# Four edits to an attention and expert kernel: an earlier Wo product, whole-tile key transposes, a head summed by parts, and weight loads queued behind gathered rows

## The chip, the cores and the metric

The kernel runs on one core of one Trainium2 chip. The metric is the device time of one execution in microseconds (us); for several runs it is their median. A core has five engines that work side by side and wait for one another by semaphores: PE (TensorE, the matrix products), DVE (VectorE), ACT (ScalarE), POOL (GpSimd) and SP (SyncE, which here only issues transfers). Transfers are issued on the queues of SP, ACT and POOL and are carried out by 16 DMA engines that all queues share.

## The reference

One layer: a linear-attention block with a data-dependent decay, then a mixture of twelve experts with two chosen per token, each with a residual and a layer norm. There are 2048 tokens of width 512, all in float32. Cut to what is computed:

```python
def attention(x):                       # heads of size 64, 8 of them
    xn = layernorm(x, gamma, beta)
    w = sigmoid(xn @ Wx @ Ww + bw)      # decay
    k, v, r = xn @ Wk, xn @ Wv, sigmoid(xn @ Wr)
    # per head, token after token:
    #   state = (1 - w_t)[:, None] * state + k_t[:, None] * v_t[None, :]
    #   y_t   = r_t @ state
    return y @ Wo

x = layernorm(x + attention(x))

def experts(x):
    probs = softmax(x @ gate_w.T)
    top_w, top_i = top_k(probs, 2); top_w /= top_w.sum()
    # out += (silu(x @ w1[e].T) * (x @ w3[e].T)) @ w2[e].T * weight of e for the token
    return out

x = layernorm(x + experts(x))
```

## The kernel before, in words

**Layout.** The tokens are taken in eight blocks of 256 (`TB`), each of two tiles of 128 rows; x stays in SBUF as `xs`. A tile has two chunks of 64 tokens (`L`), and inside a chunk the recurrence is unrolled into "levels" of block sizes 1, 2, ... 32: products of scaled queries and scaled keys, picked together by a mask. From chunk to chunk a state is carried.

**Head (lines 573 to 605).** Wx and Ww are multiplied into one matrix Wa, so that the decay needs one projection. SP first loads the first two tiles of x (line 71), then the four quarters of `ww` (line 579) in turn with `wxT` on ACT's queue (line 578), then Wk and the rest of x; Wr, Wv and Wo come on ACT's queue. PE then computes Wa by row tiles i: for each i, four quarters k, two passes each (float32 products show as two matrix instructions), into one PSUM tile that ACT copies out (line 597). So the first i already needs the last quarter. Ahead of i=2 the first block's normed rows are transposed (line 175), and after the loop a small product, `psl` (line 604), gives `lesser`, which the gate uses later.

**A block b (the loop at line 622).** PE's order is the program's order (a manual schedule for PE only); the orders on DVE, ACT, POOL and SP come from the framework's scheduler. PE does in turn: `mixed(1)` of the block before (`yp`, lines 353 and 354; ACT copies `yp` to `yT`, line 356), `levels(0)`, `residual` of the block before's second tile (`psp<-Wo,yT`, line 362; DVE adds it to `xs`, line 363, and takes statistics, lines 109 and 110), the three projections of the next block (line 197), the transposes of finished rows for the gate (`known.transpose`, line 395), `mixed(0)`, the gate's scores (`lg`, line 408), `levels(1)`, the small products of `known.place` (`pr`, line 455), `residual` of this block's first tile, the values (line 242), and the transposes of the block after next (line 175). `known.choose` is a chain of small DVE operations; `known.place` ends in indirect DMAs on POOL.

**levels (lines 288 to 343).** First the keys k64 are brought from (feature, token) to (token, feature): for each chunk c, pair of heads p and head h, a 64x64 product with the identity, into `kp` (line 296), which ACT copies to `kS` (line 300). Then 56 products per chunk give `pa` (line 316), which DVE turns into `A` (lines 318 and 321). Then `sp`, kS times the values (line 333), and two DVE operations per chunk form the new state (lines 340 and 341). `kp`, `sp` and one half of the transposes share one PSUM buffer; the projections, values, scores, `pr` and `residual` share two, in turn.

**scaled (line 255)** makes the scaled queries on DVE and ACT and the scaled keys on POOL, with two buffers per level.

**Experts (lines 801 to 958).** Experts 0 and 1 are fixed; the other ten are sorted by load and processed in that order as groups 3 to 12. Group 0 works on rows gathered during attention (`soon`), group 1 and 2 on the further rows of experts 1 and 0. Group g's body: gather the rows of group g+1 (`xg`, line 816, indirect DMAs on POOL), the hidden products (`psg`, line 845), the transposes of the gathered rows (`psx`, line 828), the output products of the group before (`pso`, line 874), each added into DRAM by an indirect DMA (line 879). The weights of one expert are a row of 2 MB; `ewp` holds three. The first two sorted experts' loads (line 929) are issued in the bodies of groups 0 and 1, later ones from group 3 on. `entries` (line 727) computes on DVE the row lists `come` of the sorted groups. At the end the sum is read back, normed and stored (lines 984 to 1000).

Of the kernel before, what the change touches and what calls it, by code (L numbers as in the profile page):

```python
# [16 lines left out]
P = 128  # L17
C = 512
# [34 lines left out]
def tile_kernel(ctx: ExitStack, tc: tile.TileContext, x, WxT, Ww, bw, Wk, Wv, Wr, Wo, gamma, beta, gate_wT, wall, same, masks, rev, cst, empty, ids, out):  # L53
# [13 lines left out]

    def load_x(i0, n):
        nc.sync.dma_start(xs[:, i0 : i0 + n, :], x[i0 * P : (i0 + n) * P, :].rearrange("(n p) d -> p n d", p=P))

    load_x(0, NTB)

    ident = const.tile([P, P], FP, tag="ident", name="ident")
    make_identity(nc, ident)
# [61 lines left out]
    with ExitStack() as att:  # L136
# [151 lines left out]
        def levels(n, S, qs, ks, vS, W):  # L288


            kp = ps_s.tile([P, 2, KT, HS], FP, tag="kp", name="kp")
            for c in range(2):
                for p in range(KT):
                    for h in range(2):
                        hp = slice(h * HS, (h + 1) * HS)
                        nc.tensor.matmul(  # L296
                            kp[hp, c, p, :], ks[L][hp, p, c * L : (c + 1) * L], ident[hp, hp], start=True, stop=True
                        )
            kS = lvl.tile([P, 2, KT, HS], FP, tag="kS", name="kS")
            nc.scalar.copy(kS, kp)  # L300

            A = []
            for c in range(2):
                cs = slice(c * L, (c + 1) * L)
                pa = ps_a.tile([P, KT, PAIRS], FP, tag="pa", name="pa")
                for p in range(KT):
                    for l in range(NL):
                        B = BLOCKS[l - 1] if l else 0
                        for h in range(2):
                            hp = slice(h * HS, (h + 1) * HS)  # L310
                            if l:
                                q = blocks(qs[B][hp, :, cs], B)[:, p, :, 1, :]
                                to = pa[hp, p, L + (l - 1) * L // 2 : L + l * L // 2].rearrange("p (i b) -> p i b", b=B)
                            else:
                                q, to = qs[0][hp, p, cs], pa[hp, p, 0:L]
                            nc.tensor.matmul(to, ks[B][hp, p, cs], q, start=True, stop=True)  # L316
                a = lvl.tile([P, KT, L], FP, tag="A", name="A", bufs=4)
                nc.vector.tensor_mul(a, pa[:, :, 0:L], eye.unsqueeze(1).to_broadcast([P, KT, L]))
                for l, B in enumerate(BLOCKS):
                    n_i = L // (2 * B)  # L320
                    nc.vector.copy_predicated(  # L321
                        blocks(a, B)[:, :, :, 1, :],
                        msk[:, l, :].rearrange("p (i b) -> p i b", b=B).unsqueeze(1).to_broadcast([P, KT, n_i, B]),
                        pa[:, :, L + l * L // 2 : L + (l + 1) * L // 2].rearrange("p q (i b) -> p q i b", b=B),
                    )
                A.append(a)

            sp = ps_s.tile([P, 2, KT, HS], FP, tag="kp", name="sp")
            for c in range(2):
                for p in range(KT):  # L330
                    for h in range(2):
                        hp = slice(h * HS, (h + 1) * HS)
                        nc.tensor.matmul(  # L333
                            sp[hp, c, p, :], kS[hp, c, p, :], vS[hp, 2 * n + c, p, :], start=True, stop=True
                        )
            states = [S]
            for c in range(2):
                new = p2.tile([P, KT, HS], FP, tag="state", name="state", bufs=6)
                whole = W[L].rearrange("p (q n) -> p q n", q=KT)[:, :, 2 * n + c : 2 * n + c + 1]
                nc.vector.tensor_mul(new, states[c], whole.to_broadcast([P, KT, HS]))  # L340
                nc.vector.tensor_add(new, new, sp[:, c, :, :])
                states.append(new)
            return A, states
# [229 lines left out]
        with ExitStack() as once:  # L573
            two = once.enter_context(tc.tile_pool(name="two", bufs=1))
            wxT = two.tile([P, KT, C], FP, tag="wxT", name="wxT")
            ww = two.tile([P, KT, C], FP, tag="ww", name="ww")
            for k in range(KT):
                nc.scalar.dma_start(wxT[:, k, :], WxT[k * P : (k + 1) * P, :])
                nc.sync.dma_start(ww[:, k, :], Ww[k * P : (k + 1) * P, :])
            load_w(nc.scalar, wsb["Wr"], Wr)  # L580
            load_w(nc.sync, wsb["Wk"], Wk)
            load_w(nc.scalar, wsb["Wv"], Wv)
            for i0 in range(NTB, NT, NTB):
                load_x(i0, NTB)
                if i0 == NTB:
                    load_w(nc.scalar, wsb["Wo"], Wo)
            xn = norm(0)
            with tc.manual_schedule(engines={PE}):
                for i in range(KT):
                    if i == 2:  # L590
                        xnT = transposed(xn)
                    ps = ps_p.tile([P, C], FP, tag="psp", name="psp")
                    for k in range(KT):
                        nc.tensor.matmul(
                            ps, wxT[:, k, i * P : (i + 1) * P], ww[:, k, :], start=(k == 0), stop=(k == KT - 1)
                        )
                    nc.scalar.copy(wsb["Wa"][:, i, :], ps)

                whole = const.tile([P, NE + NS], I32, tag="whole", name="whole")
                key, whole = whole[:, NE:].bitcast(FP), whole[:, 0:NE]  # L600
                lesser = const.tile([P, NE], FP, tag="lesser", name="lesser")
                ps = ps_p.tile([P, NE], FP, tag="psp", name="psl")
                for k in range(KT):
                    nc.tensor.matmul(ps, cc["ones"], gwT[:, k, :], start=(k == 0), stop=(k == KT - 1))
                nc.vector.tensor_scalar_mul(lesser, ps, -1.0)  # L605

        lvl = att.enter_context(tc.tile_pool(name="lvl", bufs=2))
        rt = att.enter_context(tc.tile_pool(name="rt", bufs=2))
# [4 lines left out]
        with tc.manual_schedule(engines={PE}):  # L613
# [8 lines left out]
            for b in range(NB):  # L622
                cur = kT, rT, aT, W
                tile0 = nxt
                if todo is not None:
                    yT = mixed(1, *todo)
                A0, states0 = levels(0, state, *tile0, vS, W)
                if b:
                    tile1 = scaled(1, *cur)
                else:  # L630
                    with tc.issue_after(ends[0]), tc.issue_after(ends[1]):
                        tile1 = scaled(1, *cur)
                if todo is not None:
                    residual(b * NTB - 1, yT)
                    known = Sorted((b - 1) * NTB, NTB)
                if b + 2 < NB:
                    with tc.issue_after(taken[-1]):
                        xn = norm(b + 2)
                if b + 1 < NB:
                    kT, rT, aT, W = decays_and_keys(xnT)  # L640
                    nxt = scaled(0, kT, rT, aT, W)
                ahead = b + 1 < NB
                if todo is not None and ahead:
                    known.transpose()
                yT = mixed(0, A0, states0, tile0[0][L], vS)
                if todo is not None and ahead:
                    known.score()
                    known.choose()
                A1, states1 = levels(1, states0[2], *tile1, vS, cur[3])
                state = states1[2]  # L650
                todo = A1, states1, tile1[0][L], vS
                if ahead:
                    if b:
                        known.place()
                    residual(b * NTB, yT)
                    vS = values(xnT)
                if b + 2 < NB:
                    xnT = transposed(xn)
                if b + 2 == NB:
                    proj.close()  # L660
                    soon = Soon(b * NTB)
# [139 lines left out]
    with ExitStack() as moe:  # L801
# [118 lines left out]
        groups += [Group(blocks(n), nth=r) for r, n in enumerate(SORTED)]  # L920
        weights = {(0, None): soon.w, (1, None): load_expert(1)}

        def load_sorted(r):
            if r < NS:
                weights[None, r] = w = ewp.tile([P, WROW], FP, tag="w", name="w")
                row = nc.values_load(
                    wix[0:1, r : r + 1], engines=(mybir.EngineType.SP,), min_val=0, max_val=(NE - 1) * P
                )
                nc.sync.dma_start(w, wall[bass.ds(row, P), :])

        xgT = gathered(soon.xg, groups[0].sizes)

# [3 lines left out]
        for g, group in enumerate(groups):  # L936
            ahead = groups[g + 1] if g + 1 < len(groups) else None
            if ahead:
                nxt = gather(ahead.source)
            if g < 2:  # L940
                with tc.issue_after(loaded.ins):
                    load_sorted(g)
            w = weights[group.expert, group.nth]
            h = hidden(w, xgT, group.N)
            if g == 0:
# [132 lines left out]
```

## Time and profile before

| what | us |
|---|---|
| median of 3 runs | 854.67 |
| lowest, highest | 853.89, 862.46 |
| the profiled execution, its own time | 855.35 |
| its span, first to last instruction | 853.6 |
| PE busy (share of the span) | 793.8 (93%) |
| head: first projection with Wa starts at | 26.36 |
| attention: blocks 0 to 7 up to about | 514 |
| experts: first hidden product of group 0 at | 533.31 |

How to read it: the profile is that of one execution. Its first part gives the busy time of each engine; the second cuts the span into 40 equal slices, with the share of each engine in tenths and the clock that PE was granted; the chain of waits goes back from the last instruction to what released each step, so its shares tell what set the end. Timelines list merged instructions by start, duration, engine, line, and "output<-inputs"; in square brackets stands how long the engine was idle before, and what it waited for. PE's durations of single products overlap (a product is 218 ns or more from its start to its end, while the next starts much earlier), so the pieces of the chain, not the sums of durations, are the cost of a stretch. PEld is the weight load that precedes each product.

### The profile page before, as it was taken

The numbers are of one execution on the slowest core, as the hardware profiler recorded it, in microseconds if no ns is written. First come the engines' busy times: TensorE is split into PE (matmuls) and PEld (weight loads), VectorE is DVE, ScalarE is ACT, GpSimd is POOL, SyncE is SP. The second block draws the span as 40 slices with busy tenths as digits, with TensorE's granted clock in tenths as the row PEclk, the third lists the DMA queues.
The fourth block names the chain that finished last, engine by engine and source line by source line (L and its number), as shares of the span: only waits on it lengthen the run. The fifth ranks groups of instructions, "written<-read, shape, count | busy, mean of one in ns | idle before, by whom it ended". The sixth has DMA issues, their size and how long they took to land.

```text
span 853.6 us, 18701 instructions
## 1 busy us (share of the span) xinstructions
PE 793.8 (93%) x7932; PEld 563.2 (66%) x7932; DVE 376.5 (44%) x1264; ACT 189.3 (22%) x400; POOL 247.2 (29%) x316
## 2 busy tenths in 40 slices
PE   6999999999999999999999999699999999999910
PEld 2778789789789788787886876474544544555500
DVE  2481763763665647547527456226212111111133
ACT  1231313212213213223132112011122211111104
POOL 3062302502504314224025004243243332212210
PEclk9999999999999999999999899799999999999965
DMA  9500000010010010010011224744265554645366
GB/s 331 188 2 1 3 21 32 3 51 2 3 50 2 3 50 3 3 50 3 2 51 26 102 100 141 252 104 155 56 177 135 136 130 145 162 130 137 45 198 225
DMA packets 25941, 72.78 MB, mean 85 GB/s; under 512 B 4033, under 2 KB 4193, under 8 KB 24305
## 3 DMA queue, kind: packets, MB, share of 16 engines
q1 hardware_dynamic: 14384, 48.44, 15.0%
q0 software_dynamic: 9312, 18.95, 12.0%
q10 hardware_dynamic: 2160, 4.19, 1.4%
q8 instruction: 62, 1.02, 0.5%
q14 instruction: 23, 0.18, 0.1%
HBM read 49.78 MB, written 21.99 MB: 84 GB/s over the span
## 4 chain that ended last, share of the span: by engine, by line
PE 89%; DMA 5%; DVE 2%; ACT 1%; issue 1%; ACTq 0%; POOL 0%; SPq 0%; POOLq 0%
PE psp L197 19%; PE psg L845 16%; PE pa L316 12%; PE pso L874 12%; PE psp L362 7%; PE psp L242 6%; PE psx L828 2%; PE yp L353 2%; PE sp L333 2%; PE kp L296 2%; PE yp L354 2%; PE lg L408 2%; DMA xg<-xd,src 2%; DMA xs<-in_x 2%; DVE st L109 1%; DMA acc<-y,to 1%
## 5 line engine op out<-in xcount | busy, mean ns | idle before, releaser
L845 PE MATMUL psg<-xgT,w 128*128 128x384 f32 (+4 forms) x480 | 141.0, 454 | 0.0
L845 PEld LDWEIGHTS psg<-xgT,w 128*128 128x128 f32 x480 | 91.5, 194 | 51.2 <-issue 13.9
L276 POOL TENSOR_TENSOR k<-kT,aT 128x256 f32<-128x256 f32 x16 | 16.4, 1026 | 307.0 <-ACT kT L226 228.6
L874 PE MATMUL pso<-w,h 128*128 128x512 f32 (+3 forms) x204 | 103.6, 627 | 0.0
L316 PE MATMUL pa<-q,k 64*64 64x32 f32 x2560 | 101.9, 221 | 1.3 <-issue 1.3
L316 PEld LDWEIGHTS pa<-q,k 64*64 64x64 f32 x2560 | 92.0, 137 | 1.4 <-issue 1.4
L859 DVE TENSOR_TENSOR sg<-sg,psg 128x384 f32<-128x384 f32 (+9 forms) x39 | 19.1, 490 | 157.1 <-ACT sg L857 157.1
L874 PEld LDWEIGHTS pso<-w,h 128*128 128x128 f32 (+3 forms) x204 | 31.1, 181 | 54.8 <-issue 54.0
L321 DVE COPY_PREDICATED A<-msk,pa 128x128 f32<-128x128 int32 x192 | 65.5, 341 | 3.7
L816 POOL DMA_INDIRECT xg<-xd,come x30 | 29.5, 984 | 125.6 <-PE psx L828 102.8
L879 POOL DMA_INDIRECT acc<-y,to x30 | 46.8, 1560 | 63.5 <-ACT y L878 57.5
L277 ACT COPY q<-q 128x256 f32<-128x256 f32 x96 | 40.0, 416 | 89.1 <-DVE q L275 41.2
L362 PE MATMUL psp<-Wo,yT 128*128 128x512 f32 x128 | 59.4, 607 | 0.0
L197 PE MATMUL psp<-xnT,Wa 128*128 128x256 f32 x256 | 56.8, 380 | 0.4 <-DVE lesser L605 0.4
L197 PE MATMUL psp<-xnT,Wr 128*128 128x256 f32 x256 | 56.6, 379 | 0.0
L197 PE MATMUL psp<-xnT,Wk 128*128 128x256 f32 x256 | 56.6, 379 | 0.0
L276 POOL TENSOR_TENSOR k<-k,W 128x256 f32<-128x256 f32 x80 | 54.5, 681 | 6.4
L242 PE MATMUL psp<-Wv,xnT 128*128 128x512 f32 x128 | 56.2, 592 | 0.0
L197 PEld LDWEIGHTS psp<-xnT,Wa 128*128 128x128 f32 x256 | 48.5, 190 | 9.6 <-issue 2.9
L197 PEld LDWEIGHTS psp<-xnT,Wk 128*128 128x128 f32 x256 | 48.6, 190 | 6.6
L197 PEld LDWEIGHTS psp<-xnT,Wr 128*128 128x128 f32 x256 | 48.6, 190 | 6.6
L269 DVE TENSOR_TENSOR q<-rT,aT 128x512 f32<-128x512 f32 x16 | 11.4, 711 | 79.9 <-ACT rT L232 77.7
(200 smaller groups left out, 1172.3 us busy)
## 6 DMA issues: line engine op xcount, KB each, us to landing
w<-in_wall SPq DMA_DIRECT2D x11, 2048.0 KB, 9.7
xs<-in_x SPq DMA_DIRECT2D x8, 512.0 KB, 12.3
xd<-xs SPq DMA_DIRECT2D x16, 256.0 KB, 2.5
acc<-xs SPq DMA_DIRECT2D x16, 256.0 KB, 2.6
xs<-acc SPq DMA_DIRECT2D x8, 512.0 KB, 6.4
out<-xs SPq DMA_DIRECT2D x8, 512.0 KB, 3.4
soon_w<-in_wall SPq DMA_DIRECT2D x1, 2048.0 KB
wxT<-in_WxT ACTq DMA_DIRECT2D x4, 256.0 KB, 5.4
```

Source lines behind the costliest of these rows:

```text
L197: nc.tensor.matmul(ps[:, j, :], wsb[w][:, k, m * P : (m + 1) * P], rhs[:, k, :], start=(k == 0), stop=(k == KT - 1),)
L242: nc.tensor.matmul(ps.rearrange("p q h j -> p (q h j)"), xnT[:, k, n * P : (n + 1) * P], wsb["Wv"][:, k, :], start=(k == 0), stop=(k == KT ...
L276: nc.gpsimd.tensor_mul(k_to[:, :, :, 0, :], k_from[:, :, :, 0, :], decay(B, 1))
L277: nc.scalar.copy(q_to[:, :, :, 0, :], q_from[:, :, :, 0, :])
L316: nc.tensor.matmul(to, ks[B][hp, p, cs], q, start=True, stop=True)
L321: nc.vector.copy_predicated(blocks(a, B)[:, :, :, 1, :], msk[:, l, :].rearrange("p (i b) -> p i b", b=B).unsqueeze(1).to_broadcast([P, KT, ...
L362: nc.tensor.matmul(ps, yT[:, k, :], wsb["Wo"][:, k, :], start=(k == 0), stop=(k == KT - 1))
L816: ins = nc.gpsimd.indirect_dma_start(xg[:n, j, :], None, xd[:, :], bass.IndirectOffsetOnAxis(ap=col[:n], axis=0))
L845: nc.tensor.matmul(ps[:, 0:N], w13[:, k, c0 : c0 + P], xgT[:, k, 0:N], start=(k == 0), stop=(k == KT - 1))
L859: nc.vector.tensor_mul(sg[:n, 0:N], sg[:n, 0:N], g)
L874: nc.tensor.matmul(ps[:m], h[:n, f, j * P : j * P + m], w2[:n, f, :], start=(f == 0), stop=(f == 2))
L879: add = nc.gpsimd.indirect_dma_start(acc[:, :], bass.IndirectOffsetOnAxis(ap=to[:m], axis=0), y[:m], None, compute_op=ALU.add).ins
```

## The change

1. **Head by parts.** The load of x's first rows is issued on SP behind the first quarter of `ww`. The products for Wa run with the quarters k outside and the row tiles i inside, into four accumulators at once (the two `pa` buffers, free at that time). The product for `lesser` follows quarter 1, the transposes of the first rows follow quarter 2, and the four copies to Wa follow all products.
2. **Keys by whole tiles.** `kp` is made by four 128x128 transposes, one for each pair of heads, instead of 64x64 products. Its layout is now (token of the tile, pair, head, feature), so four copies, two on DVE and two on ACT, bring the parts to `kS`, with the same layout as before.
3. **Wo product earlier.** `residual(b * NTB, yT)` of blocks 0 to 6 stands ahead of `levels(1)`, not behind it and `known.place`.
4. **First weights behind rows.** The loads of the first two sorted experts are both issued in the body of group 1, and each waits for the last gather issued till then (`queue`), that of group 2's rows.

```diff
-    load_x(0, NTB)
...
-            kp = ps_s.tile([P, 2, KT, HS], FP, tag="kp", name="kp")
+            kp = ps_s.tile([P, KT, 2, HS], FP, tag="kp", name="kp")
+            for p in range(KT):
+                nc.tensor.transpose(kp[:, p, :, :].rearrange("p h j -> p (h j)"), ks[L][:, p, :], ident)
+            kS = lvl.tile([P, 2, KT, HS], FP, tag="kS", name="kS")
             for c in range(2):
-                for p in range(KT):
-                    for h in range(2):
-                        hp = slice(h * HS, (h + 1) * HS)
-                        nc.tensor.matmul(
-                            kp[hp, c, p, :], ks[L][hp, p, c * L : (c + 1) * L], ident[hp, hp], start=True, stop=True
-                        )
-            kS = lvl.tile([P, 2, KT, HS], FP, tag="kS", name="kS")
-            nc.scalar.copy(kS, kp)
+                for h in range(2):
+                    copy = nc.scalar.copy if h else nc.vector.tensor_copy
+                    copy(kS[h * HS : (h + 1) * HS, c, :, :], kp[c * L : (c + 1) * L, :, h, :])
...
                 nc.sync.dma_start(ww[:, k, :], Ww[k * P : (k + 1) * P, :])
+                if k == 0:
+                    load_x(0, NTB)
...
+                ps = [ps_a.tile([P, 2, C], FP, tag="pa", name="psm") for _ in range(KT // 2)]
+                ps = [ps[i // 2][:, i % 2, :] for i in range(KT)]
+                for k in range(KT):
+                    for i in range(KT):
+                        nc.tensor.matmul(
+                            ps[i], wxT[:, k, i * P : (i + 1) * P], ww[:, k, :], start=(k == 0), stop=(k == KT - 1)
+                        )
+                    if k == 1:
...
+                        for n in range(KT):
+                            nc.tensor.matmul(psl, cc["ones"], gwT[:, n, :], start=(n == 0), stop=(n == KT - 1))
+                        nc.vector.tensor_scalar_mul(lesser, psl, -1.0)
+                    if k == 2:
+                        xnT = transposed(xn)
                 for i in range(KT):
-                    if i == 2:
-                        xnT = transposed(xn)
-                    ps = ps_p.tile([P, C], FP, tag="psp", name="psp")
-                    for k in range(KT):
-                        nc.tensor.matmul(
-                            ps, wxT[:, k, i * P : (i + 1) * P], ww[:, k, :], start=(k == 0), stop=(k == KT - 1)
-                        )
-                    nc.scalar.copy(wsb["Wa"][:, i, :], ps)
...
+                    nc.scalar.copy(wsb["Wa"][:, i, :], ps[i])
...
+                if ahead:
+                    residual(b * NTB, yT)
                 A1, states1 = levels(1, states0[2], *tile1, vS, cur[3])
                 state = states1[2]
                 todo = A1, states1, tile1[0][L], vS
                 if ahead:
                     if b:
                         known.place()
-                    residual(b * NTB, yT)
                     vS = values(xnT)
...
-        def load_sorted(r):
+        def load_sorted(r, after=()):
...
-                nc.sync.dma_start(w, wall[bass.ds(row, P), :])
+                ins = nc.sync.dma_start(w, wall[bass.ds(row, P), :]).ins
+                for other in after:
+                    tc.add_manual_dep(ins, other.name, SYNC, reason="rows that are needed first")
...
-            if g < 2:
+            if g == 1:
                 with tc.issue_after(loaded.ins):
-                    load_sorted(g)
+                    load_sorted(0, queue)
+                    load_sorted(1, queue)
```

## The prediction, made before the changed kernel was seen

> **What bounds the kernel now.** I read the page's engine shares first, then the chain of waits, then timelines and stage windows where the chain leaves PE.
>
> ```profile
> PE 793.8 (93%) x7932; PEld 563.2 (66%) x7932; DVE 376.5 (44%) x1264; ACT 189.3 (22%) x400; POOL 247.2 (29%) x316
> PEclk9999999999999999999999899799999999999965
> PE 89%; DMA 5%; DVE 2%; ACT 1%; issue 1%; ACTq 0%; POOL 0%; SPq 0%; POOLq 0%
> ```
>
> PE carries 89% of the chain, so time is won by giving PE less to do, or by closing its few holes; work taken off another engine wins nothing. The clock row has a 7 at slice 26: one hole is paid for twice. A steady block (b=3) in the chain, where PE goes from piece to piece without a hole:
>
> ```profile
> 204.49 1.89 PE lg L408 x16
> 206.38 1.08 PE kp L296 x32
> 207.45 6.51 PE pa L316 x224
> 213.96 0.96 PE sp L333 x32
> 214.92 0.56 PE pr L455 x4
> 215.47 3.52 PE psp L362 x8
> 219.00 6.87 PE psp L242 x16
> 225.86 0.87 PE pst L175 x8
> 229.03 0.93 PE kp L296 x32
> ```
>
> The keys' transposes, kp, cost 1.08 us (tile 1) and 0.93 us (tile 0). Eight whole 128x128 transposes, pst, cost 0.87. The two holes are the head and the first gathered group of the experts (timeline of PE):
>
> ```profile
> 6.98 5.58 PE L594 MATMUL psp<-ww,wxT 128*128 128x512 f32 x6 [6.98 <-DMA ww<-in_Ww]
> 12.83 4.56 PE L594 MATMUL psp<-ww,wxT 128*128 128x512 f32 x10 [0.26 <-DMA ww<-in_Ww]
> 548.95 1.44 PE L828 MATMUL psx<-ident,xg 128*128 128x128 f32 x4 [6.84 <-DMA xg<-xd,src]
> ```
>
> In the head PE does 6 of 32 products in 5.6 us, one pair per landed quarter of Ww. At 542.1 it stops for 6.84 us until gathered rows xg land. The windows around that stop (PEclk, DMA share and GB/s are last):
>
> ```profile
> 542.00:544.00 2.00, 0.11 (x1) 0.00 (x0) 0.41 (x1) 0.38 (x1) 0.00 (x0) 1.00 1.06 403
> 546.00:548.00 2.00, 0.00 (x0) 0.00 (x0) 0.00 (x0) 0.00 (x0) 0.00 (x0) 0.50 0.96 279
> 548.00:550.00 2.00, 1.05 (x3) 0.54 (x3) 0.00 (x0) 0.27 (x1) 0.00 (x0) 0.50 0.26 66
> 556.00:558.00 2.00, 2.00 (x8) 2.00 (x7) 1.27 (x3) 0.33 (x1) 1.37 (x2) 0.50 0.04 4
> ```
>
> The DMA engines are full until 548; the granted clock falls to 0.50 in the stop and stays there until about 558.
>
> **The change, part 1: first weights behind rows.** Before, SP issues the first two sorted experts (2 MB each) at 531.8 and 533.2, the second landing 15.3 us later, at 548.5. The four row gathers go out on POOL between 534.9 and 539.65 and PE's rows arrive when that weight does. Afterwards both loads wait for the fourth gather. What would a gather take alone? The nearest row: the two soon_xg gathers, issued 500.84 to 503.04 with nothing else moving, have their DMA traffic end at about 505.05, 2.0 us after the issue. So group 1's rows (second issue ends 537.2) land at about 539.2, and group 2's (539.65) at 541.7, even beside the two soon_y accumulations. PE needs the former at 542.1: no stop. Saved: 6.84 us. Then the clock: from 548.95 to 562.44 PE does 4 psx, 2 pso, 4 psx and 40 psg at 192 columns in 13.49 us; the same set one group later, at full clock, takes 2.60 (562.61 to 565.21) plus 6.70, 9.30. Saved: 4.19. Together **-11.0**.
> A rule that speaks against it: the Trainium skill, page "DMA: Bandwidth & Descriptors", section "Queues, rings and completion order", says each DMA engine takes turns between the queues that have work, a packet at a time. With equal turns the rows (192 x 2 KB = 0.39 MB) would get half of the 380 GB/s seen, take 2 us and land near 540 even beside the weights; the change would then be worth 0 here, since something else held PE. But the row shows them at 548.9, on the weights' heels. A queue with larger packets gets more than its half by the same rule: a weight row is 16 KB per partition against 2 KB for a gathered row, and at one part in nine of 380 (an estimate from that page) 0.39 MB takes 9.3 us from 537, to 546. I take the row.
> What is late next: the two loads now start at 541.8. They are queued on SP, where nothing but the later weight loads stands behind them (the next was at 584). 4.2 MB at 375 GB/s plus start take 12.7 us, so they land by 550 and 554.5. They are needed at 583.95-11=572.9 and about 595: hidden, with 20 us of cover. Group 3's gathers (before: 556.3 to 561, when DVE has `come`) move up to about 548 to 553 and meet the loads' end, landing by about 556; needed at 564.6.
>
> **Part 2: head by parts.** The loop over quarters goes outside, so each landed quarter feeds 8 products, not 2; x's first rows go behind the first quarter on SP. Same bytes on SP up to 6.9, so x lands there instead of at 4.85, and quarters 1 to 3 stay at about 8.6, 10.7 and 12.8 (starts of the pairs before). The first quarter is half of x's size and goes first: traffic begins at 2.0 (DMA share 0.11 in the window 0:2, 0.95 in 2:4), x took until 4.85, so it lands at 3.5 to 3.9; I take 3.9. Slow products: before, starts are 0.86 us apart (8.0, 8.8, 9.7) until about 12.0, five us after the first; after, 0.43. So until 8.9 PE does 5.0/0.86=5.8 products; the other 26.2 take 11.3; the sum for `lesser` 0.96 and the transposes 0.87: ends at 22.0, projection at 22.2 instead of 26.36: **-4.1**. Checks: quarter 1 is wanted at 9.8, quarter 2 at 14.2, quarter 3 at 18.6, all later than landing; xn is ready at 6.9+4.9=11.8 (DVE took 4.85 to 9.76) and wanted at 17.6; the last Wa copy (0.59 us) has the projection's first six products (0.22 each, 1.3 us) as cover; without that, 0.4. From both sides: -2.5 if the first quarter lands 1 us later and all its 8 products are slow, -5.4 if products are fast from the start (8.6, when quarter 1 lands, plus 24 x 0.43 and 1.83, is 20.8).
>
> **Part 3: keys by whole tiles.** Per tile, 32 64x64 products become 4 transposes: half of the pst row, 0.44. A rule against it: page "TensorE: Matmul & The Clock Gate", section "Part 4: PE-mode transpose", gives about 275 ns for one in a kernel and says that the fast clock isn't engaged for them. Four in a row at that price are 1.1 us, no gain, 16 x 0.1 us lost. Here a pst does last 272 ns, but eight end in 0.87 us since they overlap, at granted clock 1.00. I take the row. Changing between whole and 64-row products costs 0.15 (the first four yp take 0.27, later fours 0.12): kp of tile 1 pays that already (1.08), afterwards pa pays it; for tile 0 two changes are new, 0.15 before pa and some 0.1 before the transposes. Sum: 8 x (1.08+0.93) = 16.1 before; 16 x 0.44 + 16 x 0.15 + 8 x 0.1 = 10.2 after: **-5.9**. Ends: -9 with free changes, 0 by the rule's price.
> One ACT copy (0.59) becomes four, two on DVE (0.42) and two on ACT (0.37). The nearest row, vS (L252, same shape), alternates: ACT waited 15.0 us in all for the DVE copy of the same tile. So kS is whole 1.7 us after its start. It is wanted by sp, after 6.5 us of pa: hidden, costing 1 us and more per tile only if DVE begins over 4.8 us late. DVE is idle at tile 0 (5.3 us before A) and at tile 1 has `choose` in front (206.4 to 209.8) against sp at 217: cover holds.
>
> **Part 4: Wo product earlier.** The 8 products (3.5 us) are moved, not saved; their DVE add and statistics (0.68+0.68+0.17) go ahead of tile 1's A copies. They need yT, the ACT copy (0.59) after mixed. For b=1 to 6 score (1.89) lies between: yT was done at 205.98, PE arrives at 206.38; without that cover up to 1 us per block. In block 0 there is no score: mixed ends at 86.68, yT is done at 87.95: **+1.3**, once. The values' products then follow pr at once; the 3.5 us that covered A's copies, states and pr's read on DVE go. Before, DVE was busy from 213.4 to 225.2 and the pst after the values found its bank free with 1.1 us to spare. Now that backlog starts 3 us later against the values, 1.5 us shorter. DVE's order is the scheduler's, and no row shows it: between 0 and 6 x 0.9 us; I take **+1.0**, near the low end, since the q scalings in that backlog aren't wanted until the next tile 1. POOL's place DMAs keep their order and slack.
>
> **Sum.** -11.0-4.1-5.9+1.3+1.0 = -18.7: span 853.6 to 834.9. The profiled execution took 855.35 (1.75 around the span), so 836.65; the runs' median is 0.68 below it: **836.0 us**. Left as they are: the holes at 468 to 475 beside the soon_w load and the clock of 0.50 until 483 (they cost some 5 us, and may fall away or grow by 4).
>
> **Rivals.**
> (a) The rows stay late: POOL's accumulations before them, or the gathers themselves, are the slow part. For: they share POOL's queue. Against: soon_xg's 2.0 us, and the stop's end at the weights' end. 836.0+11.0 = 847.0.
> (b) DVE becomes the block's limit: 13.4 us of new copies (32 x 0.42) and a lost cover, some 1.3 us at each of 7 pst or yp: +9, 845.0. For: the 1.1 us of slack. Against: DVE idles 5.3 us after each pst.
> (c) Slower: the kS copies stand in two in-order queues and sp waits for them, at L333, in all 16 tiles. It decides from 18.7/16=1.2 us per tile, that is, copies ending 7.7 us after the transposes; at 2.5 us each the time is 836+40=876. Against: the idle DVE above.
> (d) The clock dip at 476 to 483 goes and the changes cost nothing: 836-4-3 = 829.
>
> **How the numbers follow.** Chances: likeliest 0.70 (own range 830 to 842), (a) 0.10, (b) 0.10, (c) 0.04, (d) 0.06. The range 828 to 846 takes in the likeliest, (b) and most of (d), and leaves out (a), (c) and tails. About 1% (8.5 us) is what a measurement can tell from no change; faster by that means below 846.1: likeliest, (d) and most of (b), 0.85; same, mainly (a), 0.11; slower 0.04.
>
> **What would show it.** Right: no PE idle before the first psx of xg and PEclk 1.00 at 545 to 560 of the old scale; weights issued on SP after the fourth gather; products running from 4 us; the Wa projection starting near 22; kp pieces of 0.5 to 0.6; one hole of 1.3 before the first Wo product. Wrong: a wait of PE for DMA xg, waits of sp for kS or of pst for vS, or products of Ww waiting for quarter 2.

## The result, and the profile after

The changed kernel is slower: a median of 886.08 us in four runs (881.39 to 890.96) against 854.28 for the kernel before in the same session, a ratio of 1.035 with a 95% interval of 1.027 to 1.044. The forecast was 836.0. Ratios, here and below, are taken of the runs within 1.5% of the fastest of their kernel and medians of all runs, so the two can differ: for experiment 5 below the medians make +9.9 us and the ratio +6.7. The profiled execution took 885.99 us, its span is 884.2. The mean granted clock of PE fell from 0.967 to 0.932.

The engine shares, the clock row and the chain's shares, of the page after:

```profile
PE 822.7 (93%) x7484; PEld 586.3 (66%) x7484; DVE 389.0 (44%) x1296; ACT 191.5 (22%) x416; POOL 249.2 (28%) x316
PEclk9999999999789789979969969999999999999965
PE 92%; DMA 2%; issue 2%; DVE 2%; ACT 1%; POOL 0%; SPq 0%; ACTq 0%; POOLq 0%; DVEq 0%
```

PE has 448 fewer recorded instructions than before and yet is busy 28.9 us longer. A row of shares would pass that as "93%, as before". The clock row tells it: seven of the slices 11 to 24 stand below 9, where the kernel before had a single 8 (slice 23, in block 7) in the attention. The DMA's share of the chain fell from 5% to 2% (the wait for the rows went), and "issue" doubled from 1% to 2%. In the waits of PE, the list's first two lines show where:

```profile
PE yp L350 <- issue: 6.0, 14, 1.1
PE yp L349 <- issue: 5.9, 11, 1.0
```

The columns are the time in us, the number of waits and the longest; "issue" stands for a stop for which the profile can name no releaser. There are 25 of them within the products of `yp`; before, such stops in `yp` came to 0.6 us. The chain through the same block (b=3) as was shown of before, with the first and the last of four stops in `yp`, and the pieces between left out:

```profile
209.17 0.44 PE kp L291 x4
209.61 6.65 PE pa L312 x224
...
217.78 6.96 PE psp L240 x16
...
227.15 0.36 issue
...
229.45 0.99 issue
...
230.84 0.59 PE kp L291 x4
231.43 11.85 PE pa L312 x224
243.28 1.76 PE sp L329 x32
245.04 5.49 PE psp L358 x8
```

Down to the values (L240) all is as forecast: kp 0.44, pa 6.65 with the transition in it, and sp (at 216.26) not waiting. Then `yp` takes 5.2 us (225.61 to 230.84) where it needs 2.1, and the next tile's pa takes 11.85 for the same 224 products. The windows around it (granted clock, DMA share and GB/s are last):

```profile
228.00:230.00 2.00, 0.82 (x11) 0.71 (x11) 0.00 (x0) 0.06 (x1) 1.22 (x2) 1.00 0.01 1
232.00:234.00 2.00, 2.00 (x42) 2.00 (x42) 0.43 (x1) 0.65 (x2) 0.00 (x0) 0.50 0.00 0
248.00:250.00 2.00, 2.00 (x5) 0.77 (x5) 0.00 (x0) 0.00 (x0) 0.00 (x0) 0.81 0.00 0
```

The clock is 1.00 during the stops and falls to 0.50 behind them, from about 232 to 248. So this block loses 3.1 us in yp, 5.2 in pa, 0.8 in sp and (against the 3.65 of the same product in experiment 10) 1.8 in the Wo product, 11 in all. Five blocks (3 to 7) fall so: the chain has pa at 11.85, 12.09, 12.03, 12.09 and 12.09. Block 2 has stops as well (1.8 us in sum), and its clock holds: its pa takes 6.65. Five times 7.8 (pa, sp and Wo of this block), and the 11.9 us of stops in all blocks, are 51 us; the version without them (experiment 10) has a span 52.1 us shorter.

What stands beside the stops is on POOL. Its timeline in the same block, first and last of the four place DMAs, after:

```profile
224.71 1.02 POOL L471 DMA_INDIRECT places<-pay,at  x1 [0.15 <-issue]
228.56 0.96 POOL L471 DMA_INDIRECT places<-pay,at  x1 [0.30 <-issue]
```

The last of them before, and two of PE's pieces of `yp` then:

```profile
226.28 0.96 POOL L475 DMA_INDIRECT places<-pay,at  x1 [0.30 <-issue]
```

```profile
227.77 0.47 PE L354 MATMUL yp<-A,vS 64*64 64x64 f32 x3
228.08 0.26 PE L353 MATMUL yp<-q,state 64*64 64x64 f32 x1
```

The first write comes 8.4 us after the end of levels(1)'s pa in both kernels (213.96 to 222.36, 216.26 to 224.71); that the two are equal is in part chance, since before POOL was idle for 0.76 us ahead of it, and after it follows the scaled keys at once. But yp, which began 12.8 us after that end, now begins 9.3 after it. Before, the writes ran beside the values' 512-column products, and only the last reached yp, whose groups of four break up at 228 for a moment; this could be read in the trace of before. After, three of the four writes are issued inside yp. So far this is a coincidence in time; the experiments test it.

The other parts. The first sorted rows, and the head:

```profile
575.56 8.64 PE psg L848 x40
584.20 0.78 PE psx L831 x4
```

```profile
5.18 9.40 PE L592 MATMUL psm<-ww,wxT 128*128 128x512 f32 x16 [5.18 <-DMA ww<-in_Ww]
...
23.05 3.32 PE L195 MATMUL psp<-xnT,Wa 128*128 128x256 f32 x14
```

The stop of 6.84 us ahead of the rows' transposes is gone. The head's products start at 5.18 (forecast 3.9), and its projection at 23.05 (forecast 22.2, before 26.36).

### The profile page after: what moved, and what is told of

Its sections match the earlier page's. It is cut to its first block, busy times and chain, and to the rows that moved or that the text cites. A ratio compares the mean times of both kernels' runs of the same rounds, so it can differ in the third digit from the quotient of the medians.

```text
span 884.2 us, 17861 instructions
## 1 busy us (share of the span) xinstructions
PE 822.7 (93%) x7484; PEld 586.3 (66%) x7484; DVE 389.0 (44%) x1296; ACT 191.5 (22%) x416; POOL 249.2 (28%) x316
## 3 DMA queue, kind: packets, MB, share of 16 engines
q10 hardware_dynamic: 2160, 4.19, 1.3%
## 4 chain that ended last, share of the span: by engine, by line
PE 92%; DMA 2%; issue 2%; DVE 2%; ACT 1%; POOL 0%; SPq 0%; ACTq 0%; POOLq 0%; DVEq 0%
PE psp L195 19%; PE psg L848 16%; PE pa L312 15%; PE pso L877 11%; PE psp L358 7%; PE psp L240 6%; PE yp L349 2%; PE psx L831 2%; PE sp L329 2%; PE yp L350 2%; PE psm L592 2%; PE lg L404 2%; PE kp L291 1%; DMA acc<-y,to 1%; ACT xs L1002 1%
## 5 line engine op out<-in xcount | busy, mean ns | idle before, releaser
L848 PE MATMUL psg<-xgT,w 128*128 128x384 f32 (+4 forms) x480 | 138.7, 448 | 0.0
L848 PEld LDWEIGHTS psg<-xgT,w 128*128 128x128 f32 x480 | 89.2, 190 | 51.1 <-issue 13.9
L312 PE MATMUL pa<-q,k 64*64 64x32 f32 x2560 | 116.4, 241 | 0.0
L312 PEld LDWEIGHTS pa<-q,k 64*64 64x64 f32 x2560 | 106.3, 162 | 0.0
L358 PE MATMUL psp<-Wo,yT 128*128 128x512 f32 x128 | 62.5, 633 | 1.3 <-ACT yT L352 1.3
L274 POOL TENSOR_TENSOR k<-k,W 128x256 f32<-128x256 f32 x80 | 56.6, 707 | 6.4
L240 PE MATMUL psp<-Wv,xnT 128*128 128x512 f32 x128 | 56.8, 597 | 0.0
```

Of the source, the lines that this page charges most:

```text
L240: nc.tensor.matmul(ps.rearrange("p q h j -> p (q h j)"), xnT[:, k, n * P : (n + 1) * P], wsb["Wv"][:, k, :], start=(k == 0), stop=(k == KT ...
L274: nc.gpsimd.tensor_mul(k_to[:, :, :, 0, :], k_from[:, :, :, 0, :], decay(B, 1))
L358: nc.tensor.matmul(ps, yT[:, k, :], wsb["Wo"][:, k, :], start=(k == 0), stop=(k == KT - 1))
L848: nc.tensor.matmul(ps[:, 0:N], w13[:, k, c0 : c0 + P], xgT[:, k, 0:N], start=(k == 0), stop=(k == KT - 1))
```

## The experiments

**Theory 1** (formed from the trace above): the earlier Wo product takes 3.5 us out from between `pr` and `yp`; the place DMAs therefore fall on yp (`mixed(1)`), PE stops in pieces, and the clock halves behind it. **Theory 2:** the earlier Wo product harms by its place on PE alone. **Theory 3** (theory B of experiment 5): the transposes for the keys lower what counts as work of PE, and the clock falls for that. **Rivals:** the copies to kS or DVE's order cost the time (forecast as (b) and (c)), or each part's price was wrong. All ratios are to the kernel before, on the same chip.

**1. The Wo product back where it was,** all else changed:

```diff
-                if ahead:
-                    residual(b * NTB, yT)
                 A1, states1 = levels(1, states0[2], *tile1, vS, cur[3])
...
                     if b:
                         known.place()
+                    residual(b * NTB, yT)
                     vS = values(xnT)
```

> The changed kernel with the Wo product of a block's first tile back behind the place step; the three other parts stay. Theory 1 (the place step's four indirect writes on POOL, which in the changed kernel fall on mixed(1), stop PE there in pieces, and the clock then halves for the next levels): the 3.5 us of Wo product lie between them again, so no stops in mixed(1), PEclk 1.00 in the blocks, about 836 to 842 us. Theory 2 (the earlier Wo product harms by its place on PE alone): the same 836 to 842. Theory 3 (the whole-tile transposes do not count as PE work and let the clock drop): stays near 880.

845.2 us (838.97 to 858.42), ratio 0.986 [0.980, 0.992]. The move is what costs: 1.035 against 0.986 is 42 us. The time is 3 us above the forecast and scatters. In its profile (858.42 us) there is one stop in yp, of 0.3 us, but pa behind the keys of levels(1) takes 10.97, 11.22 and 11.46 us in three blocks; experiments 5 and 8 take that up.

**2. The move alone,** on the kernel before (the same edit the other way round):

> The kernel before with the earlier Wo product alone. Theories 1 and 2: the stops of mixed(1) and the halved clock appear, 890 to 905 us (854 plus some 40 to 50). Theory 3: 854 to 856, since the keys are transposed as before.

886.83 us, ratio 1.035 [1.031, 1.040]: 3 us under the forecast. The move alone makes a loss of 30 us, as much as all four parts together; inside the changed kernel it costs 42, where five blocks fall and not three. Neither the key transposes nor the copies to kS are in this kernel, so the stops and the falls of the clock aren't theirs. Lines of its chain:

```profile
246.52 6.39 PE pa L316 x206
...
374.41 11.68 PE pa L316 x194
```

The falls don't follow from the stops alone: ahead of 246.5 there were four (2.1 us in sum), and the clock held; ahead of 374.4 there were four of 0.3 to 0.5 (1.4 in sum), and it fell.

**3. No place writes** for the tiles placed inside the attention:

```diff
-                for j, i in enumerate(self.tiles):
+                for j, i in enumerate(self.tiles if i0 >= NT - 6 else ()):
```

> The changed kernel without the 24 indirect writes of the place step of the first twelve to thirteen tiles (left out: the expert rows of those tokens are not put in the table, so the experts work on filler rows; sizes and counts of all other work stay). Theory 1: no stops in mixed(1), PEclk 1.00 in blocks 2 to 5, about 836 to 842 us. Theories 2 and 3: the stops stay, about 880 to 886.

840.53 us, ratio 0.980 [0.974, 0.987]. Blocks 1 to 6 have neither stops nor falls. Block 7, where the writes are kept, has both: its pa takes 12.05. So the Wo product's place on PE, which is unchanged here, does no harm by itself (theory 2).

**4. The same writes, later:** the place step of blocks 1 to 5 goes behind the next block's levels(0) and second Wo product, where the projections' 512-column products follow.

```diff
                 if todo is not None:
                     residual(b * NTB - 1, yT)
+                    if 1 < b < NB - 1:
+                        known.place()
                     known = Sorted((b - 1) * NTB, NTB)
...
-                    if b:
+                    if b + 2 == NB:
                         known.place()
```

> The changed kernel with the place step of blocks 1 to 5 moved behind the next block's levels(0) and second Wo product, so that its indirect writes fall on the projections; block 6 stays as it is. Theory 1: stops only in block 7's mixed(1), 842 to 850 us. Theories 2 and 3: 880 to 886.

842.84 us, ratio 0.983 [0.977, 0.989]. Nothing is left out of the work here, and the stops are gone from the blocks changed; block 7, again, keeps its own. Moving the writes is worth 44 us by the ratios, some 9 for each of the five blocks: beside the large products they leave no stop of PE. A new wait of 0.4 us appears in five blocks, for DVE's sum ahead of the projections (2.1 us).

**5 to 7. The other parts alone,** each on the kernel before: the keys by whole tiles, the weights behind the rows, the head by parts (the diffs are those parts of the change).

> The kernel before with the whole-tile key transposes alone. Theory A (the sum of the prediction: transposes are cheap and harmless): 848 to 850 us, kp pieces of 0.44 to 0.59. Theory B (the transposes count for less PE activity than the products they replace, so that the stretch transposes, mixed(0), scores, kp, with 16 products of 12 columns in it, now lets the clock fall in some blocks): levels(1) at PEclk 0.50 in one to four blocks, some 5 us each, 850 to 866 us with a wide scatter, and no hole of PE ahead of them.

> The kernel before with the first two sorted weights behind the gathered rows alone. The prediction's term: -11.0 us, so 843 to 845, no stop before the first psx of xg, both loads issued after the fourth gather. Rival (rows late for another reason): 853 to 856.

> The kernel before with the head by parts alone. The prediction's term: -4.1 us, 850 to 851; by the changed kernel's chain (projection at 23.2 instead of 26.4) -3.2 us, 851 to 852.

| part alone | median us | ratio [95%] | by the ratio, us | forecast |
|---|---|---|---|---|
| keys | 863.92 | 1.0078 [1.0053, 1.0104] | +6.7 | -5.9 |
| rows | 842.54 | 0.9864 [0.9847, 0.9880] | -11.6 | -11.0 |
| head | 851.06 | 0.9973 [0.9955, 0.9990] | -2.3 | -4.1 |

The medians are of 22, 4 and 9 runs. The keys were forecast wrong in sign. In that kernel's chain, block 2:

```profile
145.79 0.49 PE kp L293 x4
146.28 11.29 PE pa L314 x224
```

```profile
144.00:146.00 2.00, 2.00 (x19) 2.00 (x20) 1.02 (x4) 1.58 (x4) 0.00 (x0) 1.00 0.00 0
148.00:150.00 2.00, 2.00 (x42) 2.00 (x42) 0.99 (x7) 0.44 (x3) 0.00 (x0) 0.50 0.00 0
```

Here the clock falls (0.80 in the window between these two) with PE busy for the whole 2.00 of each window: no stop stands ahead of it. kp costs 0.49, as forecast; the pa behind it 11.29. The stretch ahead, from 141, is `pst` (eight transposes), yp, the gate's `lg` of 12 columns and now four more transposes. It fell in blocks 2 and 4 of this execution and not in others; runs lay between 852.6 and 875.5. The falls in the profile of experiment 1, where kp follows lg too, are of this kind. In the changed kernel the early Wo product stands between lg and kp, and no levels(1) of it fell.

**8. Keys by whole tiles in levels(0) only,** on the kernel before; there the keys follow yp, in levels(1) they follow lg.

```diff
+            if n:
                 kp = ps_s.tile([P, 2, KT, HS], FP, tag="kp", name="kp")
...
+            else:
+                kp = ps_s.tile([P, KT, 2, HS], FP, tag="kp", name="kp")
```

> The kernel before with whole-tile key transposes in levels(0) alone; levels(1), where they stood right behind the gate's narrow products and the clock fell in the kernel with both, keeps the 64x64 products. If the clock's fall there (transposes behind narrow products) is all that made the keys' part a loss: no fall in levels(1), kp of tile 0 at 0.59 instead of 0.93 and pa up 0.15, so 8 x 0.2 = 1.6 us less, 852 to 853, ratio 0.996 to 0.999. If something else of the edit costs (the four copies, or whole-tile transposes anywhere): about half of the loss stays, 857 to 859, ratio above 1.003.

849.83 us, ratio 0.9935 [0.9915, 0.9955]: a gain, and no pa above 6.65 in the chain. It is larger than the 1.6 expected, since block 7's fall of the kernel before (its chain: a stop of 1.25 us that splits a pa whose two parts take 8.5 in place of 6.5, then sp at 1.76 and the Wo product at 4.14) didn't come either. So the copies and the transposes cost nothing in levels(0); in levels(1), behind lg, they do.

**9. Which property of the writes?** The changed kernel, the indirect writes of those tiles replaced by direct ones of the same 128 rows of 8 bytes, first on SP's queue, then on POOL's:

```diff
-                for j, i in enumerate(self.tiles):
+                for r in range(12 if i0 < NT - 6 else 0):
+                    nc.sync.dma_start(scr[(i0 // 2) * 12 + r], at[:, 2, 2 * (r % 2) : 2 * (r % 2) + 2])
+                for j, i in enumerate(self.tiles if i0 >= NT - 6 else ()):
```

> The changed kernel, but the place step of blocks 1 to 5 (as in the kernel without place writes) issues no indirect writes from POOL; SP issues twelve direct writes of 128 rows of 8 bytes in their stead, to a scratch array in DRAM, as soon as the small table they come from is ready. Left out: the row lists of those tiles' tokens. If the small packets in flight stop PE, this is slow again: PE's pieces of 0.3 to 1.1 us in yp, pa of 11.9 us, some 880 us. If the issuing on POOL's queue (or the form, indirect) is needed, the time is that without writes, 840.

> The changed kernel, with the indirect writes of the place step of blocks 1 to 5 replaced by eight direct writes of 128 rows of 8 bytes each on POOL's queue, to a scratch array in DRAM. Left out: the row lists of those tiles' tokens. If issuing small writes on POOL is what stops PE, direct or not: some 870 to 886 us with pieces in yp. If it is the indirect form alone: 840, without pieces. Only this one slow, and not the one with SP's writes: POOL's making of the descriptors. Both fast: the indirect form. Both slow: the packets.

839.22 us (0.981 [0.977, 0.984]) and 837.02 us (0.981 [0.978, 0.984]): the time is that without writes. On POOL's queue the eight writes lie right on yp, and yp runs through. POOL, then the first and last groups of yp:

```profile
220.75 4.30 POOL L471 DMA_DIRECT2D scr<-at  x8
```

```profile
221.78 0.34 PE L350 MATMUL yp<-q,state 64*64 64x64 f32 x4
...
223.58 0.33 PE L351 MATMUL yp<-A,vS 64*64 64x64 f32 x4
```

SP's writes lie on yp in block 4 (twelve of them from 281.32 to 287.19, yp from 283.75 to 285.88), and yp runs through there, too; in block 3 none is issued while yp runs. By the expectations this would say that it takes the indirect form. It doesn't, for two reasons that the same traces show.

First, both kernels keep the four indirect writes of block 6, which fall on yp of block 7, just as in experiment 3. POOL's first write, and the chain with the first of four stops in yp, in experiment 3:

```profile
459.45 1.07 POOL L471 DMA_INDIRECT places<-pay,at  x1 [0.19 <-issue]
```

```profile
459.57 0.27 PE yp L349 x4
...
461.11 0.37 issue
```

and with direct writes on POOL's queue in the blocks before it:

```profile
461.31 1.08 POOL L474 DMA_INDIRECT places<-pay,at  x1 [0.17 <-issue]
```

```profile
461.44 0.27 PE yp L350 x4
...
463.38 0.12 PE yp L351 x4
463.50 0.59 PE kp L292 x4
```

The first write starts 0.13 us ahead of yp and the second 1.25 us into it (in experiment 3 0.12 and 1.25, and the first stop stands 1.54 us into it), and yet PE doesn't stop in yp. With SP's writes it is the same: the two start at 464.62 and 466.00, yp runs from 465.11 to 467.17 without a stop. So something else that both edits change counts, too. One thing that they share is the scratch array (64 KB), which is allocated ahead of `places`, the array that the indirect writes go to. Whether that matters wasn't tested.

Second, the direct writes are not without stops. Outside of block 7 PE stops within pa or sp for 1.7 us in sum with POOL's writes and for 4.4 with SP's, again with no releaser named, where experiment 10 has no such stop; the clock didn't fall there. So which property of the writes stops PE in yp stays open.

**10. A version without the collision:** experiment 4, with block 6's Wo product put back behind its place step.

```diff
-                if ahead:
+                if b + 2 < NB:
                     residual(b * NTB, yT)
...
                     if b + 2 == NB:
                         known.place()
+                        residual(b * NTB, yT)
```

> The changed kernel with the place step of blocks 1 to 5 moved behind the next block's second Wo product, as before, and in block 6 the Wo product back behind the place step. If the place writes on mixed(1) are what halves the clock in block 7, its hole goes as well: 833 to 837 us. If the load of the first expert's 2 MB, which falls on the same place, is enough for that, 840 to 843 as in the kernel with block 6 unchanged.

833.82 us (832.57 to 837.99), ratio 0.977 [0.975, 0.979]: faster than both kernels, and as expected if the place writes make block 7's hole. Its clock row has no digit below 9 ahead of the end:

```profile
PEclk9999999999999999999999999999999999999965
```

and behind yp in block 3 the chain runs as the prediction had it:

```profile
224.52 0.59 PE kp L291 x4
225.11 6.65 PE pa L312 x224
```

**11. That version with the old 64x64 keys:**

> The fastest version so far (place later, block 6 back; 833.8 us, ratio 0.9768 to the kernel before), with the keys brought over by 64x64 products as before. If the whole-tile transposes are worth what the prediction gave them (5.9 us) where nothing pulls the clock down, this takes 839 to 840, ratio 0.983 to 0.984. If they are worth nothing or harm by themselves (alone on the kernel before they made it 0.8% slower), it takes 834 or less.

843.4 us, ratio 0.9871 [0.9853, 0.9889], 3 us above the expectation. The whole-tile keys are worth 8.8 us here by the ratios. About 4 of them are a fall of the clock in block 7, which this kernel has and the other not:

```profile
472.14 1.74 issue
473.88 5.42 PE pa L314 x106
```

The rest agrees with the chain: kp 1.08 and 0.93 against 0.44 and 0.59, pa 6.51 against 6.65 twice, 0.7 us a block, 5.6 for eight.

## Why the prediction was wrong, point by point

**The step that failed** is the end of part 4: "POOL's place DMAs keep their order and slack." The order was kept. The slack was the 3.5 us of Wo product and the tolerance of the products behind it, and both were given away: the prediction followed those 3.5 us for DVE (A's copies, the states, pr's bank) but not for POOL, whose chain follows pa and not the Wo product, and so didn't move with PE (the first write stands 8.4 us behind pa's end in both traces, and three of the four are now issued inside yp). What it cost: 11.9 us of stops in yp and, with the clock at 0.50 behind them, some 7.8 us more in each of five blocks. Removing the writes, moving them, or putting the product back each takes the loss away (experiments 1, 3 and 4), and the move alone makes it (2). That the two meet is needed for the loss in these kernels, but it isn't all: in block 7 of both kernels of experiment 9 they meet without a stop. No rival held it: the one for slower was the wait of sp for kS, which never came. A rival "what lies beside the dense products when they come 3.5 us earlier" would have had its price in the same profile: the clock of 0.50 after the stop at 542 was priced there at 4.19 us, and a fall of that kind in each block of six is 25 us and more.

**Part 3, keys.** The price of a piece was right (0.44 to 0.59 against 0.44 and some 0.15 of transitions), and so was the hiding of the copies. What failed is the choice of row against rule. The page "TensorE: Matmul & The Clock Gate", section "Part 4: PE-mode transpose", says that transposes don't count as busy PE in the same way; the prediction set that aside because a pst ran at granted clock 1.00. That row shows only that eight transposes behind large products leave the clock alone. Experiment 5, with four more of them behind narrow products, agrees with the rule: the clock fell to 0.50 with PE busy, and it cost 6.7 us where a gain of 5.9 was forecast. That it is the way transposes are counted which brings it down is argued, not shown. In the surroundings of the changed kernel the forecast of -5.9 holds (5.6 by the chain of experiment 11).

**Part 1, rows:** right in size, and by half in mechanism. -11.6 alone against -11.0; the loads now wait on SP for the last gather (583.89, the gather at 580.82), and PE meets its rows. That POOL's queue gets little beside the weights is in the trace of before. The DMA queues in 534 to 544 (q1 is SP's, q0 POOL's; packets, MB, share), and q0 in 544 to 550:

```profile
q1 hardware_dynamic: 226, 3.44, 85.7%
q0 software_dynamic: 168, 0.31, 17.2%
```

```profile
q0 software_dynamic: 266, 0.79, 44.9%
```

That is one part in 12, near the one in nine of the prediction, where equal turns would give half. But the rows didn't trickle in from 537 to 546, as it had it: 0.79 MB is the size of all four gathers (384 rows of 2 KB), so they moved only as the weights ran out. What moved slowly beside the weights were the accumulations issued ahead of them on POOL's queue. Rival (a) was thus right about the queue, but without the weights beside them those took 4.8 us from issue to landing (experiment 6). That the estimate of 546 came near 548.9 is in part luck.

**Part 2, head:** right in mechanism, short in size: -2.3 (between -3.8 and -0.9) against -4.1, a little short of the small end of its bounds (-2.5). In the profile of the head alone the projection starts at 22.13, as forecast (22.2), with the first quarter landed at 4.38 in place of 3.9. In the changed kernel that quarter landed at 5.18, and the projection starts at 23.05, 3.3 us earlier than before and not 4.1; so the term that scatters is the landing. The sixteen products behind it took 9.3 to 9.4 us, as the prediction's rates make it. What is missing from the time of the head alone, with its projection on time, wasn't found.

**Part 4's own prices:** the wait of block 0 for yT was forecast at 1.3 and is 1.3. The cost of DVE's order was put at 1.0; in the changed kernel PE's waits for DVE are those of before (0.7 and 0.2 us), so it was nothing. The 2.1 us of experiments 4 and 10, at the projections, come with the moved place step: experiments 3 and 9 don't have them.

**The sum.** 836.0 is nearly what experiment 10 takes, 833.8, but not by the same terms. From 854: rows -11.6, head -2.3, keys -5.6, block 7's fall gone about -4 (rival (d)), yT +1.3, the wait with the moved place step +2.1, together -20.1. The terms are taken from different runs, so that they meet the 833.8 so closely is in part luck. (Rival (d) takes off 3 us for changes that cost nothing, where the sum has only 2.3 of cost; nothing hangs on it.)

**Still open:** how the place writes stop PE, why they don't in block 7 of experiment 9, and why stops of the same size bring the clock down in one block and not in another (block 2 of the changed kernel, experiment 2). That stops stand ahead of these falls, and that both go when the writes or the move go, was shown.

## What to carry to other kernels

When an instruction is moved ahead of others, list what every other engine does at that time, on the old and on the new scale: work that doesn't hang on the moved piece stays where it was, and what it lay beside is now something else. Price the clock with each gap or stretch of narrow products on PE: here a loss of 2 us in pieces cost 8 more behind it. And where small transfers fall on a train of small products, try them beside large ones: here that was worth 44 us (experiment 4). And when an experiment is to tell which property of a thing does the harm, look in its trace for a place where the thing was kept: experiment 9 gives a clean answer by its times, and block 7 of it takes the answer back.

## What the runs showed of the hardware that was not expected

- PE stopped in every one of the 14 blocks of the changed kernel and of experiments 2, 3 and 4 in which three or four indirect writes (128 rows of 8 bytes each) on POOL lay on yp, while it issued 64x64 products at about 30 ns each. It didn't in the two such blocks of experiment 9, so the writes alone don't make the stops. Beside 512-column products (222 to 226 in the profile before) they left none.
- The stops aren't one for each write. In block 3 the writes were 1.3 us apart, the stops ended at 227.50, 228.25, 228.98 and 230.44, that is, at steps of 0.73 or twice that, with three to six products between; in all 14 blocks the first stop came after 45 to 48 of the 64 products of yp. It looks like a supply in portions behind a store. What is supplied wasn't shown.
- Stops of 1.3 to 2.2 us in sum within some 3 us came ahead of a fall of the clock to 0.50 in ten of the 14 blocks; in one it fell in part (pa 7.21), in three it held. It then stayed at 0.50 for some 16 us of wholly busy PE in block 3, through pa and sp, and rose during the 512-column products that followed (0.81 in 248 to 250).
- The clock also fell with PE busy in every window, behind transposes and 12-column products (experiment 5).
